# Opening and second group of a fused two-layer transformer step: blank products, spare buffers, loads and norm steps in other places

## The chip, the cores and the metric

The kernel runs on one core of a Trainium2 chip. A core has five engines with a queue of instructions each: TensorE (PE, matrix products; its weight loads are shown as PEld), VectorE (DVE), ScalarE (ACT), GpSimd (POOL) and SyncE (SP, which here only starts DMA transfers). The engines wait for each other through semaphores; within one queue the order is the order of the program. The metric is the device time of one execution in microseconds, lower is better. The kernel before takes 899.39 us (median of three runs, 898.83 to 901.31).

## What is computed

The reference takes x (64 sequences of 32 rows, width 256) and a context (64 x 257 rows) through two layers. Layer 0, where the change lies, is:

```python
x = x + _L0_xattn_ref(_layernorm(x, axis=-1), ctx_1024, ctx_1024, ...)   # windowed attention on the context
x = x + _L0_attn_ref(_layernorm(x, axis=-1), ...)                        # causal attention on x itself
x = x + _L0_ffn_ref(_layernorm(x, axis=-1), ...)                         # FP8 linear
```

Both attentions have 16 heads of 16 features and a rotary turn of queries and keys; each of the 32 query rows of a sequence sees at most 32 keys, so a layer 0 attention touches only the first 32 context rows. Layer 1 (attention on all 257 context rows, a gated mixer, and a mixture of experts) follows and isn't touched by the change.

## The kernel before, in words

The 2048 rows of x lie in four groups of 512 rows (`xs[0]` to `xs[3]`), each of four tiles of 128 rows. The function `small_attentions` runs both layer 0 attentions as eight steps, n = 0 to 7: the context attention of groups 0 to 3, then the self attention of groups 0 to 3. In this text "step n, tile t" is one turn of the inner loop. A turn does a piece of several jobs at once, so that PE always has something: it scores tile t of group n (`scores`), transposes and uses the exponentials of older tiles (`turned`, `context`, `by_feature`, `project`, on tiles one to four turns old), and prepares the next group `after`: `rotated` makes half of its keys (t = 0, 1) or queries (t = 2, 3), `values` its values (t = 0, 2).

`rotated` is the rotary turn: PE makes `ps_qk`; DVE makes `part` (sine part), SP starts four DMA transfers that move `part` by 32 partitions into `far`, `near` (cosine part) is made by ACT and POOL (by DVE in step 0's own opening), and POOL adds `near` and `far` into kT or qT. `spread_keys` copies kT into the block form `kb`. `v_rows`, `vb` carry the values through DRAM; `blocks` starts eight transfers a group.

The norm of a group is the generator `norm_steps`: statistics (`st`, four DVE instructions), aggregation (`mv`, then `ve`, `half`, `r`), three Newton rounds for the reciprocal root (`sq`, `rn`: nine small DVE instructions, or twelve on POOL), and four DVE instructions that write y. Its argument `eng` says which engine does the Newton rounds. Each `next` on the generator runs up to the next `yield`. `opened` transposes y on PE (eight `psT` products) and copies it with ACT into yT. Before the change, step n's loop works through the norm of group n + 2 in its four turns (`prepare`), with the Newton rounds on DVE for n = 0 and on POOL for n > 0, and opens that group in turn 3.

The order on every engine is the order of the program text in this part (`tc.keep_in_program_order`), and the rings of named buffers (`ring`) decide when a buffer comes free: `part` has two buffers, `near` two, `far` three, the PSUM banks of `pa` three. A DMA transfer also waits for the earlier transfer with the same one of eight semaphores.

The opening is what stands ahead of the loop: loads of x, weights, constants and context on SP's queue (`first_loads`), the norms of groups 0 and 1, the four rotations and the values of group 0.

Of the kernel before, what the change touches and what calls it, by code (L numbers as in the profile page):

```python
# [16 lines left out]
P = 128  # L17
# [48 lines left out]
def perceiver_kernel(ctx: ExitStack, tc: tile.TileContext, a: dict, out: bass.AP):  # L66
# [57 lines left out]
    def norm_steps(g, eng=None, apart=False, ts=range(NT), by_act=False, y=None):  # L124
# [18 lines left out]
        r = r0.bitcast(F32)  # L143
        for _ in range(3):
# [103 lines left out]
    def small_attentions(layers, first_loads, decode, sides, load_layer1, layer1):  # L248
# [30 lines left out]
        def clear(vb, engine):  # L279
            engine.memset(vb.rearrange("p b h g e -> p (b h g e)"), 0.0)  # L280
# [25 lines left out]
        def rotated(it, i, c):  # L306
# [19 lines left out]
            part = part_([P, GT], "part")  # L326
# [8 lines left out]
            near = near_([P, GT], "near")  # L335
# [166 lines left out]
        last = len(order) - 1  # L502
        in_order[0] = all_in_order[0] = True
# [9 lines left out]
        next(loads)  # L513
        for half in range(2):
            clear(vbs[0][half], vector)
            clear(vbs[1][half], gpsimd)
# [4 lines left out]
        adds = [rotated(it, 1, 0)]  # L521
        opened(it)
        mask(1)
        vector.tensor_tensor(eye, ident[:, 0:S], ident[:, 64 : 64 + S], ALU.add)
        steps = norm_steps(order[1][1], vector, apart=True)
        next(steps)
        adds.append(rotated(it, 1, 1))
# [4 lines left out]
        adds.append(rotated(it, 0, 1))  # L532
        adds[1]()
# [6 lines left out]
        after["y"] = finish(steps)  # L540
        for half in range(2):
            blocks(it, half)
        now = it


        line = [None] * 5
        adds = []
        layer1_loads = load_layer1()
        for n in range(len(order) + 1):
# [4 lines left out]
            kvT = coming = None  # L554
            if n + 2 <= last:
                side = norm_steps(order[n + 2][1], None if n else vector, apart=True)
            else:
                side = sides

            def prepare(at):  # L560
                if n + 2 <= last and at:
                    try:
                        next(side)
                    except StopIteration as end:
                        return end.value

            for t in range(NT):
# [12 lines left out]
                if t == 0:  # L580
# [11 lines left out]
                else:  # L592
                    y = prepare(t % 2 == 1)
                    adds.append(rotated(after, *((1, 0), (1, 1), (0, 0), (0, 1))[t]))
                    if (n, t) == (last - 1, NT - 1):
# [3 lines left out]
                prepare(t % 2 == 0)  # L599
# [6 lines left out]
                if n > 0 and (t % 2 == 0 or n + 2 > last):  # L606
# [7 lines left out]
                elif t % 2 == 0:  # L614
                    values(after, t // 2)
                    if (n, t) == (0, 0):
                        opened(after)
                elif t == 3:
                    for half in range(2):
                        blocks(after, half)  # L620
                    if n + 2 <= last:
                        coming = group(n + 2, kvT)
                        coming["y"] = y
# [1515 lines left out]
```

## Time and profile before

| what | value |
| --- | --- |
| median of three runs | 899.39 us (898.83 to 901.31) |
| profiled execution, its own time | 899.84 us |
| its span, first to last instruction | 898.1 us |
| mean granted TensorE clock | 0.984 |
| PE busy | 852.6 us (95%) |
| DVE busy | 577.4 us (64%) |
| POOL busy | 508.9 us (57%) |
| first scores read by DVE (`mx`, step 0, tile 0) | 33.33 us |
| step 1 from its first `part` (50.87) to that of step 2 (74.74) | 23.87 us |

Times are counted from the start of the span. The windows view gives busy time of each engine in a stretch and the clock that TensorE was granted; the chain of waits follows the last instruction back to the start and says for each stretch who set the end; the timeline lists instructions in order of time with their durations. Matrix products are pipelined, so PE's busy share counts waiting inside a product too.

### The profile page before, as it was taken

The numbers are of one execution on the slowest core, as the hardware profiler recorded it, in microseconds if no ns is written. First come the engines' busy times: TensorE is split into PE (matmuls) and PEld (weight loads), VectorE is DVE, ScalarE is ACT, GpSimd is POOL, SyncE is SP. The second block draws the span as 40 slices with busy tenths as digits, with TensorE's granted clock in tenths as the row PEclk, the third lists the DMA queues.
The fourth block names the chain that finished last, engine by engine and source line by source line (L and its number), as shares of the span: only waits on it lengthen the run. The fifth ranks groups of instructions, "written<-read, shape, count | busy, mean of one in ns | idle before, by whom it ended". The sixth has DMA issues, their size and how long they took to land.

```text
span 898.1 us, 22831 instructions
## 1 busy us (share of the span) xinstructions
PE 852.6 (95%) x8699; PEld 585.8 (65%) x8699; DVE 577.4 (64%) x1702; ACT 439.7 (49%) x1135; POOL 508.9 (57%) x990
## 2 busy tenths in 40 slices
PE   6899999987989999999999999999999889999996
PEld 3466666664556666666566665666676548888885
DVE  6887777895576767775787757776765861111116
ACT  2566667673455545555455554665653232222224
POOL 3477777773584657557475573685661254555430
PEclk9899999999999999999999999999998999999998
DMA  7455433543101111110111101120010056777768
GB/s 237 134 141 141 99 95 96 132 134 111 48 8 54 54 55 54 54 40 16 54 55 54 45 12 53 55 71 25 2 37 1 24 159 216 232 233 229 217 191 284
DMA packets 66926, 88.77 MB, mean 99 GB/s; under 512 B 32480, under 2 KB 50688, under 8 KB 64768
## 3 DMA queue, kind: packets, MB, share of 16 engines
q1 hardware_dynamic: 63264, 77.73, 28.8%
q0 software_dynamic: 3456, 9.44, 3.2%
q8 instruction: 69, 1.13, 0.6%
q14 instruction: 41, 0.34, 0.1%
q10 hardware_dynamic: 96, 0.13, 0.1%
HBM read 65.78 MB, written 13.11 MB: 88 GB/s over the span
## 4 chain that ended last, share of the span: by engine, by line
PE 72%; DVE 11%; POOL 6%; ACT 4%; issue 4%; DMA 3%; SPq 1%; DVEq 0%; POOLq 0%; ACTq 0%
PE ps_v L119 12%; PE ps_o L119 11%; PE ps_k L119 10%; PE ps_h L119 7%; PE ps_t L122 7%; PE ps_qk L119 5%; PE ps_s L119 3%; PE ps_p L119 3%; PE ps_so L119 2%; PE pair_bank L119 2%; PE ps_sh L119 2%; PE ps_q L119 2%; POOL sq L107 1%; POOL e L107 1%; ACT e L107 1%
## 5 line engine op out<-in xcount | busy, mean ns | idle before, releaser
L107 ACT ACTIVATE e<-e,xnm 128x257 f32<-128x257 f32 x256 | 127.2, 499 | 44.1 <-DVE xnm L107 39.5
L119 PE MATMUL ps_k<-ct,w_w_l1x 128*128 128x512 f32 x256 | 122.9, 602 | 3.5 <-DMA ct<-in_ctxT 2.4
L107 POOL TENSOR_SCALAR e<-e,xsm 128x256 f32<-128x256 f32 x256 | 124.2, 504 | 0.0
L107 DVE CUSTOM_DVE_ANT_0 e<-ps_s,mask 128x257 f32<-128x257 f32 x256 | 93.5, 421 | 43.7 <-PE ps_s L119 43.1
L119 PE MATMUL ps_v<-w_w_l1x,ct 128*128 128x256 f32 x512 | 121.1, 379 | 0.0
L122 PE MATMUL ps_t<-cst,e 128*128 128x128 f32 x640 | 102.1, 282 | 2.9 <-DVE eT L107 2.8
L119 PEld LDWEIGHTS ps_v<-w_w_l1x,ct 128*128 128x128 f32 x512 | 93.4, 190 | 10.9 <-ACT y L107 0.2
L107 DVE COPY eT<-ps_t 128x512 f32<-128x512 f32 x124 | 85.1, 686 | 23.4 <-PE ps_t L122 23.2
L107 ACT ACTIVATE kT<-ps_k,vec 128x512 f32<-128x512 f32 x64 | 44.0, 688 | 100.1 <-PE ps_k L119 100.1
L107 POOL TENSOR_TENSOR x<-x,rows 128x256 f32<-128x256 f32 x96 | 70.3, 750 | 34.5 <-DVE y L107 25.2
L122 PEld LDWEIGHTS ps_t<-cst,e 128*128 128x128 f32 x640 | 71.8, 141 | 20.8 <-DVE eT L107 4.4
L107 ACT ACTIVATE hTr<-ps_h,w 128x256 f32<-128x256 f32 (+1 forms) x80 | 31.4, 450 | 104.2 <-issue 90.5
L107 DVE TENSOR_TENSOR og<-ps_o,b 128x512 f32<-128x512 f32 (+1 forms) x20 | 12.8, 638 | 105.6 <-PE ps_o L119 105.6
L119 PEld LDWEIGHTS ps_k<-ct,w_w_l1x 128*128 128x128 f32 x256 | 44.6, 190 | 44.7 <-issue 36.8
L1882 POOL DMA_INDIRECT r_rows<-og,lv x36 | 35.6, 989 | 59.1 <-DVE og L107 54.2
L107 ACT COPY v<-ps_v 128x512 f32<-128x512 f32 x80 | 46.5, 582 | 41.6 <-PE ps_v L119 41.0
L119 PE MATMUL ps_h<-ygT,w 128*128 128x256 f32 (+1 forms) x320 | 65.8, 359 | 0.1
L119 PE MATMUL ps_o<-w,hTr 128*128 128x256 f32 x288 | 65.3, 379 | 0.0
L107 POOL TENSOR_TENSOR last<-e,xsm 128x4 f32<-128x4 f32 x64 | 15.4, 240 | 88.0 <-DVE xsm L107 86.5
L119 PEld LDWEIGHTS ps_o<-w,hTr 128*128 128x128 f32 x288 | 54.4, 190 | 7.2
L119 PEld LDWEIGHTS ps_h<-ygT,w 128*128 128x128 f32 x320 | 54.9, 190 | 6.2 <-issue 0.3
L107 ACT ACTIVATE kb<-kT,cst 128x256 f32<-128x256 f32 x96 | 45.4, 512 | 27.5 <-POOL kT L107 25.9
(223 smaller groups left out, 1668.9 us busy)
## 6 DMA issues: line engine op xcount, KB each, us to landing
ct<-in_ctxT SPq DMA_DIRECT2D x16, 1024.0 KB
w<-in_ew SPq DMA_DIRECT2D x20, 514.0 KB
w<-in_ew SPq DMA_DIRECT2D x20, 512.0 KB
far<-part SPq DMA_DIRECT2D x126, 64.0 KB
v_rows<-v SPq DMA_DIRECT2D x16, 256.0 KB
vb<-v_rows SPq DMA_DIRECT2D x64, 64.0 KB
r<-r_rows SPq DMA_DIRECT2D x8, 512.0 KB
b<-in_eb SPq DMA_DIRECT2D x20, 128.0 KB
```

What stands on the lines that cost most here:

```text
L107: ins = getattr(self.engine, name)(*args, **kw)
L119: return kept(nc.tensor.matmul(ps, **args))
L122: return kept(nc.tensor.transpose(ps, src, eye))
L1882: wrote = nc.gpsimd.indirect_dma_start(out=r_rows, out_offset=bass.IndirectOffsetOnAxis(ap=write_i[:, at : at + 1], axis=0), in_=o[:, i, : ...
```

## The change

The opening: a `blank` tile of zeros is written by DVE and 14 products of it are put ahead of PE's first real product. DVE's two clearings of `vb` go to POOL, which now clears all four. Both key rotations of group 0 come before `opened`, and they take their `part` and `near` from the tiles of the scores and exponentials (`spare`). The load of group 2's rows and of the last weight block moves from SP's queue early on to ACT's queue behind the second mask, that of group 3's rows and of one bias row to step 0, tile 2. The Newton rounds and y of group 1 come behind the query rotations (`split`).

The norms: group 2 does only its statistics in step 0 and the rest in step 1, turns 0 and 1, where it is opened; group 3 (in step 1) has its Newton rounds on DVE instead of POOL, its pieces in turns 1, 2 and 3. Group 1 is opened in step 0, turn 1 instead of turn 0. In step 0 the pending additions (`add`) come at the start of every turn. The fetch of group 2's context and one piece of the FP8 decoding come a turn or two later. From step 2 on the order of the turns is that of before.

```diff
...
     def turn(ps, src, eye):
...
-    def norm_steps(g, eng=None, apart=False, ts=range(NT), by_act=False, y=None):
+    def norm_steps(g, eng=None, apart=False, ts=range(NT), by_act=False, y=None, split=False):
...
         n, t0 = len(ts), ts[0]
...
         r0 = small.tile([P, n], I32, tag="r0", name="r0")
...
         r = r0.bitcast(F32)
+        if split:
+            yield
         for _ in range(3):
...
             rn = small.tile([P, n], F32, tag="rn", name="rn", bufs=6)
...
             scalar.copy(mk, cst[:, at : at + S][:, None, :].to_broadcast([P, 8, S]))
...
-        def clear(vb, engine):
-            engine.memset(vb.rearrange("p b h g e -> p (b h g e)"), 0.0)
+        def clear(vb):
+            gpsimd.memset(vb.rearrange("p b h g e -> p (b h g e)"), 0.0)
...
             layer, g = order[n]
...
                 return tile_.rearrange("p (b q) -> p b q", q=S)
...
             bias = vec[:, v0 + 2 * i + c : v0 + 2 * i + c + 1]
-            part = part_([P, GT], "part")
+            spare = (it["n"], i) == (0, 1)
+            part = sb.tile([P, GT], F32, tag=f"sc{c}", name="part") if spare else part_([P, GT], "part")
             vector.scalar_tensor_tensor(
...
             )
...
             for at in range(0, P, S):
...
                 queue.dma_start(out=far[at : at + S, :], in_=part[at ^ S : (at ^ S) + S, :])
-            near = near_([P, GT], "near")
+            near = sb.tile([P, GT], F32, tag=f"e{c}", name="near") if spare else near_([P, GT], "near")
             if it["n"] > 0:
...
                 gpsimd.tensor_tensor(by_seq(near), by_seq(near), by_place(cs), ALU.mult)
...
         last = len(order) - 1
+        blank = sb.tile([P, GT], BF16, tag="e2", name="blank")
+        vector.memset(blank, 0.0)
+        idle = psum.tile([P, GT], F32, tag="b5", name="idle")
+        for _ in range(14):
+            mm(idle, lhsT=blank[:, 0:P], rhs=blank, start=True, stop=True)
         in_order[0] = all_in_order[0] = True
...
         it = group(0, fetch(0))
...
         after = group(1, fetch(1))
-        next(loads)
-        for half in range(2):
-            clear(vbs[0][half], vector)
-            clear(vbs[1][half], gpsimd)
+        for vb in vbs[0] + vbs[1]:
+            clear(vb)
         scalar.copy(ident_bf, ident)
...
         it["kb"] = [None, None]
-        adds = [rotated(it, 1, 0)]
+        adds = [rotated(it, 1, c) for c in range(2)]
         opened(it)
         mask(1)
+        next(loads)
         vector.tensor_tensor(eye, ident[:, 0:S], ident[:, 64 : 64 + S], ALU.add)
-        steps = norm_steps(order[1][1], vector, apart=True)
+        steps = norm_steps(order[1][1], vector, apart=True, split=True)
         next(steps)
-        adds.append(rotated(it, 1, 1))
+        next(steps)
         adds[0]()
...
         adds.append(rotated(it, 0, 1))
+        next(steps)
         adds[1]()
...
             spread_keys(it, 0, 1, part)
...
             add()
...
             values(it, pair)
-        after["y"] = finish(steps)
         for half in range(2):
             blocks(it, half)
+        after["y"] = finish(steps)
         now = it
-
         line = [None] * 5
-        adds = []
+        adds, side = [], None
         layer1_loads = load_layer1()
...
             if n > 0:
...
             if after is not None:
...
             kvT = coming = None
+            earlier = side
             if n + 2 <= last:
-                side = norm_steps(order[n + 2][1], None if n else vector, apart=True)
+                side = norm_steps(
+                    order[n + 2][1], None if n > 1 else vector, apart=True, split=n == 0
+                )
             else:
...
-            def prepare(at):
-                if n + 2 <= last and at:
+            def prepare(count):
+                y = None
+                for _ in range(count if n + 2 <= last else 0):
                     try:
...
                     except StopIteration as end:
-                        return end.value
+                        y = end.value
+                return y
+
+            ahead, behind = {
+                0: ((0, 0, 0, 0), (0, 0, 1, 0)),
+                1: ((0, 0, 0, 1), (0, 1, 1, 0)),
+            }.get(n, ((0, 1, 0, 1), (1, 0, 1, 0)))
...
                 if (n, t) == (last + 1, 2):
...
                     elif after is not None:
...
                 due, adds = adds, []
-                if t == 0:
+                if t == 0 or n == 0:
                     for add in due:
...
                     due = []
...
                 if after is None:
...
                 else:
-                    y = prepare(t % 2 == 1)
+                    if n == 1 and t == 0:
+                        next(earlier)
+                    elif n == 1 and t == 1:
+                        after["y"] = finish(earlier)
+                    y = prepare(ahead[t])
                     adds.append(rotated(after, *((1, 0), (1, 1), (0, 0), (0, 1))[t]))
+                    if n < 2 and t == 1:
+                        opened(after)
                     if (n, t) == (last - 1, NT - 1):
...
                     by_feature(line[3])
-                prepare(t % 2 == 0)
+                prepare(behind[t])
+                if (n, t) == (1, 0):
+                    next(earlier)
                 if n + 2 > last:
...
                     add_bias(n - 1, t)
-                if n > 0 and (t % 2 == 0 or n + 2 > last):
+                if n > 0 and (n, t) != (1, 0) and (t % 2 == 0 or n + 2 > last):
                     next(decode, None)
...
                     add()
...
                     next(layer1, None)
...
                     values(after, t // 2)
-                    if (n, t) == (0, 0):
-                        opened(after)
                 elif t == 3:
...
                         coming = group(n + 2, kvT)
-                        coming["y"] = y
-                        opened(coming)
+                        if n > 0:
+                            coming["y"] = y
+                            opened(coming)
                 line[0] = scores(now, t) if n <= last else None
...
                     pair_pool.close()
...
                     sums(line[1])
...
                     next(side, None)
-                if t == 0 and n + 2 <= last:
+                if (n, t) == (1, 0):
+                    next(earlier)
+                elif (n, t) == (1, 2):
+                    prepare(1)
+                if t == (0 if n else 1) and n <= last - 2:
                     kvT = fetch(n + 2)
-                elif n < 3:
+                elif n < 3 and (n, t) != (0, 0):
                     next(loads, None)
...
                     next(layer1_loads, None)
...
             sync.dma_start(out=w_cur[:, i], in_=a["w_l0x"][:, i])
...
         yield
-        sync.dma_start(out=xs[2], in_=x_view[2])
-        sync.dma_start(out=w_cur[:, 3], in_=a["w_l0x"][:, 3])
+        scalar.dma_start(out=xs[2], in_=x_view[2])
+        scalar.dma_start(out=w_cur[:, 3], in_=a["w_l0x"][:, 3])
+        yield
+        sync.dma_start(out=xs[3], in_=x_view[3])
         row_load(R_XO0)
-        sync.dma_start(out=xs[3], in_=x_view[3])
         yield
         sync.dma_start(out=raw, in_=a["w_fp8"])
-        for at in (R_AO0, R_FF, R_XO1, R_GO):
+        row_load(R_AO0)
+        for at in (R_FF, R_XO1, R_GO):
             yield
```

## The prediction

> **What bounds the kernel now.** I read the page's busy times first, then busy time by stretch, then the chain of waits, then the timeline at the places that the change moves.
>
> ```profile
> PE 852.6 (95%) x8699; PEld 585.8 (65%) x8699; DVE 577.4 (64%) x1702; ACT 439.7 (49%) x1135; POOL 508.9 (57%) x990
> ```
>
> PE sets the time almost everywhere, so only time in which PE has nothing to do, or runs at half clock, can be won. The next view has step 1 and step 2, each from its first `part` to that of the next step (columns: PE, weight loads, DVE, ACT, POOL busy, granted clock, DMA share, GB/s).
>
> ```profile
> 50.87:74.74 23.87, 23.23 (x370) 16.09 (x369) 20.02 (x45) 15.79 (x37) 17.93 (x29) 1.00 0.53 131
> 74.74:98.57 23.83, 23.50 (x370) 16.01 (x369) 18.41 (x44) 16.25 (x37) 17.14 (x29) 1.00 0.54 138
> ```
>
> The reader is to see that step 1 has 0.64 us of idle PE, but that DVE, the engine to which the change sends work, is at 20.02 of 23.87, with 3.85 us left, and POOL at 17.93.
>
> ```profile
> 26.50:30.00 3.50, 1.39 (x7) 0.64 (x5) 3.29 (x12) 0.00 (x0) 0.69 (x2) 0.99 0.58 167
> 30.00:33.40 3.40, 2.51 (x45) 1.76 (x46) 1.44 (x6) 2.93 (x6) 1.74 (x2) 0.50 0.57 134
> 33.40:36.80 3.40, 3.40 (x4) 0.90 (x4) 3.06 (x15) 1.03 (x2) 0.00 (x0) 0.50 0.65 190
> ```
>
> After a stretch with PE at 40% the granted clock is half for 6.8 us. The chain of waits has what that and the opening cost:
>
> ```profile
> 13.70 5.26 DMA far<-part
> ...
> 27.20 2.95 issue
> ...
> 33.20 3.71 PE ps_qk L119 x4
> ...
> 38.18 1.72 PE ps_qk L119 x4
> ```
>
> The first `far` needs 5.26 us, behind rows that nobody needs yet. ACT then waits 2.95 us at 27.20 for the `part` of group 1, which stands on DVE behind group 1's Newton rounds and y. The same four products take 3.71 us at half clock and 1.72 later. The timeline shows what holds those rounds, DVE first, then POOL:
>
> ```profile
> 24.09 0.16 DVE L107 SCALAR_TENSOR_TENSOR sq<-sq,ve 128x4 f32<-128x4 f32 x1
> 24.29 1.24 DVE L107 SCALAR_TENSOR_TENSOR rn<-sq,r 128x4 f32<-128x4 f32 x1
> 25.56 1.19 DVE L107 TENSOR_TENSOR sq<-rn 128x4 f32<-128x4 f32 x1
> 26.79 0.41 DVE L107 SCALAR_TENSOR_TENSOR sq<-sq,ve 128x4 f32<-128x4 f32 x1
> 27.23 0.16 DVE L107 SCALAR_TENSOR_TENSOR rn<-sq,rn 128x4 f32<-128x4 f32 x1
> ```
>
> ```profile
> 24.24 2.49 POOL L107 TENSOR_TENSOR qT<-near,far 128x512 f32<-128x512 f32 x2 [1.48 <-DMA far<-part]
> 26.71 0.48 POOL L107 TENSOR_SCALAR kb<-kT,cst 128x256 f32<-128x256 f32 x1
> ```
>
> A Newton instruction of 0.16 us that meets a POOL instruction ends with it: 1.24 and 1.19 us beside the two additions, 0.41 beside `kb`. Just one passes between two POOL instructions. In step 1 POOL is full right behind the `part` that ends at 51.62:
>
> ```profile
> 51.83 0.47 POOL L107 TENSOR_SCALAR kb<-kT,cst 128x256 f32<-128x256 f32 x1
> 52.51 1.28 POOL L107 TENSOR_TENSOR near<-near,cst 128x512 f32<-128x512 f32 x1 [0.21 <-ACT near L107]
> 53.74 0.92 POOL L107 TENSOR_TENSOR x<-x,rows 128x256 f32<-128x256 f32 x1
> 54.64 0.48 POOL L107 TENSOR_SCALAR kb<-kT,cst 128x256 f32<-128x256 f32 x1
> ```
>
> **The opening, up to the first scores.** DVE's clearings (two of 1.76 us) go. Group 0's statistics start at 5.06 behind them; SP's issue at 4.75, which waits for the landing of the same rows, says that they could start 0.3 us earlier. From there to y's end the trace takes 5.42 us. POOL now clears four times 1.81 us, to 7.97, and `ve`, `half`, `r` come at 6.4. No row has such a DVE instruction beside a clearing: 0 if they pass, 1.6 if they wait to 7.97; the nearest row, a y of 0.69 instead of 0.35 us beside a POOL addition, waits, but that addition reads and a clearing doesn't, so I take the middle, 0.8. y ends at 11.0 (10.2 to 11.8; before 10.48).
>
> By the Trainium skill, "SBUF — State Buffer", "Who interferes with whom", the first to issue of a two-port DVE instruction and any GpSimd instruction holds the shared ports to its end; these three could be such instructions, and by it the sum would be 0.8 us worse. No row here shows it.
>
> DVE then has two `part` and two `near` of the keys (4 x 0.67), eye, statistics, aggregation (2.4), and `part`, `near`, `part` of the queries (2.0): the last ends at 18.1 instead of 21.80. The 14 blanks run beside all this: PE is free until the context's rows land (6.89). Each lies between 0.27 us (bf16 128x256, warm) and 0.86 (f32 128x512, half clock); at 0.43, half of the latter, they end at 7.6 and delay keys that DVE reads from 11.0: nothing. Cover gone (0.86 each, to 13.6), up to 2.6 us.
>
> On the queues, ACT issues group 2's rows and the weight block behind its second mask copy at about 14; with some 3.5 us to landing (step 0's context, issued at 34.72, landed so) that is 17.5, and SP's first `far` of the queries reuses that transfer's semaphore. Then four issues and two of 0.63 us, 1.6 to landing (issue ends 48.93, addition starts 50.58), and POOL's second addition of 1.27: qT is there at 24.5, the second half of the scores (0.35) and `mx` at 24.9. Group 1's `r` can meet POOL's first kT addition, up to 1.27; I take 0.8 and have `mx` at 25.7 instead of 33.33. Bounds 24.9 and, with y's 0.8 more, 27.
>
> From there to the first `part` of step 1 PE has 15.7 us at the full-clock rows (four turns: `ps_qk` 1.72 four times, `ps_v` 1.73, scores 0.69 three times, group 1's eight `psT` 0.97, and the small ones). Two new waits come, the second `psT` bank and `ps_qk` for yT, both on ACT: 1.3 and 0.9; eight hand-overs of 0.05 make 0.4. Before, the same stretch took 17.54 with 2 us of half clock and group 2's `psT`. `part` comes at 43.9 instead of 50.87: **-7.0** (-5 to -8.5).
>
> **Step 1.** Call that `part` P. In turn 0: part 0.67; nine Newton instructions at 0.20, 1.8; their waits, each POOL instruction holding one of them (rest of qT's addition 0.3, kb 0.47, near 1.28, x 0.74, kb 0.48): 3.3. mx, sc, o, sums: 2.63; y 0.67, x 0.30, y 0.67. y ends at P+10.0. PE stands before the second half of `psT`; then `psT` 0.48, `ps_c` 0.22, scores 0.69; behind part and group 3's statistics `mx` comes at P+12.0, before at P+7.6: 4.4 lost.
>
> In turn 1 to 2: ACT's near, two yT and cT behind `part` (P+10.7) end at P+13.1, `ps_p` and `ps_qk` at 15.7, part 16.4, aggregation 17.3, Newton 1.8 plus near 1.28, x 0.74, kT 1.28, kb 0.5, less the 0.3 that overlaps: 22.6; the CAST 0.29 (its 1.22 at 52.85 ends 0.28 behind POOL's near). `mx` at P+22.9, before P+14.7. Turn 3 and the first of step 2: mx to y 4.27, `psT`, scores 1.2, ps_o to scores 6.4: P+34.8, before P+26.6. Step 1 loses **+8.2**, of which 6.8 are POOL's holds. 3.4 us of Newton on POOL go, which hid at all but 0.64 us.
>
> PE now stands twice for about 3 us. After 40% busy the row above has half clock. If a low stretch follows here, PE's work of a turn (5 to 6 us) takes up to 3.4 us more, twice, partly beside DVE: 0 to 5, I take **+2.5**. By the Trainium skill, "TensorE: Matmul & The Clock Gate", "What's actually happening", a whole idle window of about 3.4 us is needed, so that stands of 3 us would cost nothing and the sum be +1.2; the row at 26.50, 1.39 of 3.50 busy, speaks against it.
>
> From step 2 on the turns are those of before and PE is full: nothing moves. The later decode step and loads are hidden: DVE has 5 us free in step 2, and the eighth product's weights come in step 4. Sum: -7.0 + 8.2 + 2.5 = +3.7. The profiled execution's own time is 899.84 (span 898.1; 0.45 above the median): **903.5 us**.
>
> **Rivals.** (1) The lead stays. If POOL stands behind a late `far` while DVE does its rounds, they pass at 0.20 each; then step 1 loses the added work alone, 8.2 - 6.8 = 1.4, plus 0.8 for the clock, and the sum is -4.8: 895.0. For it: POOL is idle 6 us of 23.87, and qT's addition waited 0.72 for `far` at 50.58. Against it: near and x follow every `part` within 1.6 us. It decides once the holds fall under 3.0 us. (2) No clock loss: -7.0 + 8.2 = +1.2, 901.0. For it: the two stands are shorter than the 3.5 us stretch. (3) The opening gives half: y waits, and ACT's load lands late, so the queries' `far` stand on SP: -4.5 + 8.2 + 4 = +7.7, 907.5, with half clock in the opening as well.
>
> **How the numbers follow.** Forecast 44%, (1) 27%, (2) 14%, (3) 15%. What a measurement can tell here is about 0.3%, 2.7 us: faster is below 896.7, slower above 902.1. (1) gives faster 0.25 and the rest same; (2) gives same with a quarter slower; the forecast and (3) give slower but for 0.03: faster 0.25, same 0.16, slower 0.59. Range 894.0 to 908.5, which leaves out the best of (1) and the worst of (3); the forecast's own is 901.5 to 907.
>
> **What would show it.** First `mx` at 25 to 27; no half clock near 30; Newton instructions of 0.4 to 1.3 us on DVE in step 1; step 1 (first `part` to the next step's) 32 to 35 us instead of 23.87, with PE idle for about 3 us before `psT` in turn 1 and before `ps_c` in turn 3; windows of 0.50 behind these. Wrong if step 1 stays under 27 us, or if the first scores come after 29.

## The result, and the profile after

The changed kernel takes 904.74 us (median of nine runs, 902.43 to 908.38) against 899.44 us; the ratio is 1.0061, with a 95% interval of 1.0041 to 1.0082. It is slower, by about 5 us. The profiled execution took 903.56 us, with a span of 901.8 us. Its busy times, from the page:

```profile
PE 859.8 (95%) x8713; PEld 589.2 (65%) x8713; DVE 580.9 (64%) x1710; ACT 439.3 (49%) x1135; POOL 508.1 (56%) x980
```

The page's sums tell little, so busy time by stretch is to be read. Step 1 and step 2 of the changed kernel, each from its first `part` to that of the next step (columns as in the prediction):

```profile
45.87:75.45 29.58, 24.68 (x373) 16.12 (x372) 25.84 (x67) 16.76 (x38) 15.00 (x17) 1.00 0.43 110
75.45:99.67 24.22, 23.50 (x370) 16.02 (x369) 19.43 (x44) 16.28 (x38) 18.21 (x29) 1.00 0.52 142
```

Step 1 grew from 23.87 to 29.58 us: DVE is busy for 25.84 of it (before 20.02), and PE has 4.9 us to spare instead of 0.64. The granted clock is 1.00, so in this execution none of it is the clock. The stretch that had the half clock before:

```profile
26.50:30.00 3.50, 3.01 (x23) 1.60 (x12) 2.82 (x5) 2.54 (x6) 1.27 (x1) 1.00 0.38 88
30.00:33.40 3.40, 2.87 (x50) 1.66 (x49) 2.23 (x4) 3.40 (x8) 0.00 (x0) 1.00 0.55 127
33.40:36.80 3.40, 2.89 (x50) 1.89 (x48) 2.06 (x5) 0.94 (x3) 1.97 (x3) 1.00 0.58 157
```

The half clock there is gone. Where the time went, in four readings of DVE's timeline:

| | before | changed | difference |
| --- | --- | --- | --- |
| first scores read (`mx`, step 0, turn 0) | 33.33 | 27.30 | -6.0 |
| first `part` of step 1 | 50.87 | 45.87 | -5.0 |
| first `part` of step 2 | 74.74 | 75.45 | +0.7 |
| first `part` of step 3 | 98.57 | 99.67 | +1.1 |
| end of the span | 898.1 | 901.8 | +3.7 |

The opening wins 5 us, step 1 loses 5.7, step 2 another 0.4. The rest comes late: from 250 us on both kernels run the same instructions in the same order on PE, DVE, ACT and POOL, and yet 1.7 us are lost near 617 and 1.8 near 710, while 0.8 come back between 200 and 250 us. At both places the changed kernel's clock records have a half-clock window more (3.41 us each). The profiles of the experiments show that such windows come and go though the work there is the same (last section). So this trace places only 1.1 of the 3.7 us in the steps that the change touches.

The chain of waits of this trace reaches back only to 892.95 us, so the waits view has to stand for it. For PE from 26 to 76 us, the three longest (who waited for whom; us in total, times, longest):

```profile
PE ps_c L122 <- DVE o L107: 1.9, 1, 1.9
PE pair_bank L119 <- POOL qT L107: 1.8, 1, 1.8
PE psT L122 <- DVE y L107: 0.9, 2, 0.7
```

Before, PE had three such waits (1.5, 1.5 and 0.6 us), in step 0 and behind turn 1 of step 1. The first of the new ones is DVE's fourth-group rounds in turn 2 of step 1. The timeline there, POOL and DVE together:

```profile
61.40 1.27 POOL L107 TENSOR_TENSOR near<-near,cst 128x512 f32<-128x512 f32 x1 [2.19 <-ACT near L107]
61.47 1.23 DVE L107 TENSOR_TENSOR sq<-r 128x4 f32<-128x4 f32 x1
...
63.31 1.27 POOL L107 TENSOR_TENSOR kT<-near,far 128x512 f32<-128x512 f32 x1
63.41 1.19 DVE L107 SCALAR_TENSOR_TENSOR rn<-sq,r 128x4 f32<-128x4 f32 x1
```

Each of these rounds starts behind the beginning of a POOL instruction and ends with it; the one between them, beside POOL's `x`, takes 0.65 us. The scores of that turn lie ready in PSUM from 62.4 on and are read at 66.21. The second wait, of 1.8 us, is another thing: a qT addition at 47.85 that waited 2.44 us for `far`, because the load of group 3's rows was put at 40.97 among the small transfers. The DMA view from 40 to 50 us (KB each, median us from issue to landing):

```profile
x<-in_x SPq DMA_DIRECT2D x1, 512.0 KB
...
far<-part SPq DMA_DIRECT2D x4, 64.0 KB, 4.5
```

From 30 to 34 us, with no load beside it, the same view gives 2.0 for a `far`. An experiment further down bears out that the load is the cause: with it elsewhere PE's wait for qT falls from 1.8 to 0.2 us.

### The profile page after: what moved, and what is told of

Its sections match the earlier page's. It is cut to its first block, busy times and chain, and to the rows that moved or that the text cites. A ratio compares the mean times of both kernels' runs of the same rounds, so it can differ in the third digit from the quotient of the medians.

```text
span 901.8 us, 22853 instructions
## 1 busy us (share of the span) xinstructions
PE 859.8 (95%) x8713; PEld 589.2 (65%) x8713; DVE 580.9 (64%) x1710; ACT 439.3 (49%) x1135; POOL 508.1 (56%) x980
```

## Experiments

All ratios are to the kernel before, run on the same chip in the same series; brackets hold 95% intervals. "Turn" is a turn of the step's inner loop, `mx` the moment at which DVE reads that turn's scores.

### The two halves of the change by themselves

The opening alone: the changed kernel's opening, loads and additions, with the norms in the loop as before.

```diff
-                side = norm_steps(
-                    order[n + 2][1], None if n > 1 else vector, apart=True, split=n == 0
-                )
+                side = norm_steps(order[n + 2][1], None if n else vector, apart=True)
...
-            ahead, behind = {
-                0: ((0, 0, 0, 0), (0, 0, 1, 0)),
-                1: ((0, 0, 0, 1), (0, 1, 1, 0)),
-            }.get(n, ((0, 1, 0, 1), (1, 0, 1, 0)))
+            ahead, behind = (0, 1, 0, 1), (1, 0, 1, 0)
...
-                        if n > 0:
-                            coming["y"] = y
-                            opened(coming)
+                        coming["y"] = y
+                        opened(coming)
...
```

> The changed kernel's opening, loads and additions, with the norms of the steps as they were before (third group's whole norm in step 0 on VectorE, fourth group's Newton rounds on POOL in step 1). Theory A (the opening wins 6 us and the moved norms lose 7 in step 1): first scores read by VectorE at 27.3 as in the changed kernel, first part of step 2 at 92.5 to 94 instead of 98.57, time 894 (ratio 0.994). Rival B (what the opening wins is lost again by step 2 whatever the norms do, since step 0 then waits for its loads): first scores at 27.3, first part of step 2 within 1 us of 98.57, time 899.4 (ratio 1.000). Rival C (the blank products and the earlier start put one or two more half-clock windows behind step 8, 3.5 us in the profile of the changed kernel, whatever the steps do): steps as by A, but time 897.5 (ratio 0.998).

Measured: 904.62 us, ratio 1.0039 [1.0013, 1.0065]. First scores at 28.77. The expectation's reading has to be mended: its 98.57 is the kernel before's first `part` of step 3, not of step 2, and 92.5 to 94 was meant for that one. It came at 101.95 (and that of step 2 at 77.77, 3.0 later than before), so none of the three holds. It isn't a clean half, either. Group 2's rounds now stand in turn 1 in front of a `part`, and group 1's yT, which ACT copies behind that `part`, is late:

```profile
PE ps_qk L119 <- ACT yT L107: 3.9, 1, 3.9
```

```profile
30.64:34.06 3.42, 0.93 (x28) 0.49 (x15) 2.98 (x14) 0.91 (x3) 0.00 (x0) 1.00 0.53 121
34.06:37.47 3.41, 2.03 (x3) 1.00 (x4) 1.72 (x4) 3.41 (x8) 1.90 (x3) 0.50 0.61 163
```

PE stands 3.9 us (first view: waits), and the clock is half for 6.8 us behind that (second: windows). By turn 2 the whole lead of 4.6 us is gone. So rival B in another form: here the opening's gain does not outlast the group 2 norm that DVE has to do in step 0.

The norms alone: the opening and the loads of before, with the changed kernel's norms in the loop.

> The opening and loads of before, with the changed kernel's norms in the steps. Theory A: the moved norms alone lose 7 us between the first scores of step 0 and those of step 2 (43.5 to 45 us there in the kernel before, 51.27 in the changed one), time 906.5 (ratio 1.008). Rival B (the loss in the changed kernel belongs to the early start, for example to transfers that are not there yet, and not to the norms): the same stretch within 1.5 us of that before, time 899 to 901 (ratio 1.000 to 1.002). Rival D (the loss is half and half): 903 (1.004).

Measured: 909.25 us, ratio 1.0078 [1.0046, 1.0110]; from the first scores of step 0 to those of step 2 51.86 us (before 44.12, changed 51.27). So between those readings the norms cost 7.7 us with the opening of before, and 7.2 with the changed one: theory A's 7 us whatever the opening does, and rivals B and D fall. Half clock is part of these numbers (3.4 us of that stretch before, 8.9 here, none in the changed kernel), so they are no pure price of DVE's work. The time is above theory A's 906.5. The rounds are held here as in the changed kernel (1.27, 0.41 and 1.22 us in turn 0; 1.23, 0.66, 1.19 in turn 2). The profile has the half clock behind turn 2's stand as well, which the changed kernel's has not:

```profile
68.90:72.31 3.41, 1.53 (x5) 0.39 (x3) 3.24 (x10) 0.72 (x2) 0.21 (x1) 1.00 0.15 46
72.31:75.72 3.41, 2.73 (x33) 1.88 (x40) 2.62 (x8) 1.45 (x4) 0.00 (x0) 0.50 0.00 0
```

### Another engine: the rounds on POOL

Both groups', and then the fourth group's alone:

```diff
-order[n + 2][1], None if n > 1 else vector, apart=True, split=n == 0
+order[n + 2][1], None, apart=True, split=n == 0                      # both
+order[n + 2][1], None if n else vector, apart=True, split=n == 0     # the fourth group's alone
```

> The changed kernel with all Newton rounds of the third and fourth group on POOL (12 instructions of 0.2 us a group), in the same places of the order. Theory A in its prediction's form (POOL's holds on VectorE's Newton instructions are most of the loss, about 5 us of long instructions in the profile of the changed kernel): mx of turn 2 of step 1 at about 61 to 62 instead of 66.21, time 899.5 to 901 (ratio 1.000 to 1.002). Rival E (it is the place of the norms, not the engine: statistics, rounds, y and transposes of the third group all in step 1 have to pass in a row): no gain, 904.5 (ratio 1.006); where POOL is full, even 906.

> The changed kernel with the fourth group's Newton rounds alone on POOL, as before; the third group's stay on VectorE in step 1. Theory A: turn 2 of step 1 is freed of 1.8 us of work and some 2.5 us of holds on VectorE, turn 0 keeps its own; mx of turn 2 comes 3 to 4 us earlier than 66.21, time 901 (ratio 1.002). Rival E (place, not engine): 904.5 (1.006). Rival F (POOL's rounds of the fourth group stand behind its near, x and kT additions and come no sooner than VectorE's): mx of turn 2 at 65 to 66, 904.

Measured: 905.34 us, 1.0041 [1.0018, 1.0063], and 904.75 us, 1.0036 [1.0008, 1.0064]. With both groups on POOL `mx` of turn 2 comes at 64.93, not at theory A's 61 to 62, and the time is rival E's. The second run shows why taking the rounds off DVE doesn't give the time back. `mx` of turn 2 comes at 62.45, the 3.8 us earlier that theory A said. But the next turn, from there to its own `mx`, takes 8.1 us instead of 5.6:

```profile
65.92 0.20 POOL L107 TENSOR_TENSOR rn<-sq,rn 128x4 f32<-128x4 f32 x1
66.07 0.72 POOL L107 TENSOR_TENSOR x<-x,rows 128x256 f32<-128x256 f32 x1
66.15 2.06 DVE L107 TENSOR_SCALAR y<-x,mv,rn 128x256 f32<-128x256 f32 x2 [1.08 <-POOL rn L107]
66.75 1.31 POOL L107 TENSOR_TENSOR kT<-near,far 128x512 f32<-128x512 f32 x1
```

Twelve rounds on POOL end at 66.12, y waits for them, is itself held by the two POOL instructions behind (2.06 instead of 0.64 us), and the transposes of turn 3 wait for y. Of 3.8 us, 1.2 are left at the first `part` of step 2 (74.26). So rival E has a share: the changed kernel begins this norm a turn later than the kernel before did, and no engine has room to catch up.

### Other places

Group 2's norm back into step 0, in its turns 1 to 3, and group 3's with the rounds on POOL, as before:

```diff
-                    order[n + 2][1], None if n > 1 else vector, apart=True, split=n == 0
+                    order[n + 2][1], None if n else vector, apart=True, split=n == 0
...
-                0: ((0, 0, 0, 0), (0, 0, 1, 0)),
-                1: ((0, 0, 0, 1), (0, 1, 1, 0)),
+                0: ((0, 0, 1, 0), (0, 1, 1, 0)),
...
-                if (n, t) == (1, 0):
-                    next(earlier)
-                elif (n, t) == (1, 2):
-                    prepare(1)
+                if (n, t) == (0, 3):
+                    prepare(1)
+                elif (n, t) == (1, 0):
+                    after["y"] = finish(earlier)
```

> The changed kernel with the third group's statistics in turn 1, its Newton rounds in turn 2 and its first y at the end of turn 3 of step 0 (all on VectorE), the second y in turn 0 of step 1, and the fourth group's norm as before: statistics in turn 0, rounds on POOL in turn 1, y in turns 2 and 3. Theory E (it is the places: in the changed kernel the third group's rounds stand before the scores of turn 0, and the fourth group's norm begins a turn later than before and is late for the transposes of turn 3): first part of step 2 at 71 to 72.5 instead of 75.45, time 900.5 to 901.5 (ratio to before 1.000). Rival A2 (VectorE has no room in step 0 either, step 0 gets longer by what step 1 gets shorter): first part of step 1 at 48 to 49 instead of 45.87, that of step 2 at 74 to 75.5, 904 (1.004).

Measured: 903.31 us, 1.0028 [1.0007, 1.0049]. Step 1 takes 25.07 us, 4.5 less than in the changed kernel, but begins at 50.73 instead of 45.87, and step 2 at 75.80: rival A2, a little beyond its own figures. The nine rounds in turn 2 of step 0 take 5.6 us instead of 1.8, and six of them are held; behind that stand the clock is half from 42.3 to 49.2 us, which has its part in step 1's late begin:

```profile
36.63 1.24 DVE L107 SCALAR_TENSOR_TENSOR rn<-sq,r 128x4 f32<-128x4 f32 x1
...
38.10 1.12 DVE L107 SCALAR_TENSOR_TENSOR sq<-sq,ve 128x4 f32<-128x4 f32 x1
...
39.70 1.21 DVE L107 TENSOR_TENSOR sq<-rn 128x4 f32<-128x4 f32 x1
```

### Loads, blank products, clearing

The loads of groups 2 and 3 and of the last weight block together on SP, behind the queries' last `far`:

```diff
         mask(1)
-        next(loads)
...
         adds.append(rotated(it, 0, 1))
+        next(loads)
...
-        scalar.dma_start(out=xs[2], in_=x_view[2])
-        scalar.dma_start(out=w_cur[:, 3], in_=a["w_l0x"][:, 3])
-        yield
+        sync.dma_start(out=xs[2], in_=x_view[2])
+        sync.dma_start(out=w_cur[:, 3], in_=a["w_l0x"][:, 3])
         sync.dma_start(out=xs[3], in_=x_view[3])
+        yield
```

> The changed kernel with the third and fourth group's rows and the last weight block issued together on SP behind the queries' last far, instead of on ACT at 13.5 and on SP at 41. Theory G (large transfers that land between the small far ones cost the changed kernel part of its gain: far takes 4.1 to 4.6 us there instead of 1.4, the first kT addition starts at 18.75 when its last far lands at 18.73, and in turn 0 of step 1 PE stands 1.8 us for a qT addition whose far takes 3.1 to 3.5 us): first kT addition at 16.5, first scores read at 25 to 25.7 instead of 27.30, mx of turn 0 of step 1 at 46 to 47 instead of 49.73, time 2 to 3.5 us below the changed kernel, 902 (ratio to before 1.001). Rival H (VectorE's y of the second group and its Newton rounds bound the first scores anyway, and what is won is lost in step 1 to the norms): first scores at 27, part of step 2 within 1 us of 75.4, 904.7 (1.004 to 1.005).

Measured: 909.51 us, 1.0113 [1.0081, 1.0145], the slowest of all. Half of theory G is right: first scores come at 25.73, so the loads at 13.5 do cost the changed kernel's opening 1.6 us. But these 1.25 MB now lie in front of the writes of v to DRAM, and ACT can't refill v:

```profile
30.57 0.59 ACT L107 COPY v<-ps_v 128x512 f32<-128x512 f32 x1 [3.18 <-DMA v_rows<-v]
```

PE waits 3.4 us for that copy, and turn 1 takes 6.9 us instead of 3.6. Neither place was free. This run shows one thing more. In step 1 the last qT addition waits only 0.75 us for its `far` (2.44 in the changed kernel), POOL is busy while DVE does its rounds in turn 0, and five of the nine are held, for 3.0 us together; PE stands before `psT` in turn 1 and before `ps_c` in turn 3, and the clock is half behind both (waits, then the windows at the first stand; at the second they are 70.64 to 77.46):

```profile
PE psT L122 <- DVE y L107: 2.9, 2, 2.2
PE ps_c L122 <- DVE o L107: 1.9, 1, 1.9
```

```profile
53.58:56.99 3.41, 1.19 (x4) 0.18 (x3) 3.31 (x10) 1.51 (x3) 0.00 (x0) 1.00 0.65 178
56.99:60.40 3.41, 3.41 (x50) 2.35 (x51) 2.87 (x8) 1.74 (x4) 0.97 (x1) 0.50 0.66 183
```

Step 1 takes 32.65 us here.

Both of these edits, with the second pair of buffers cleared in turn 0 of step 0:

> Both of these edits, and the clearing of the second pair of buffers moved from the start to turn 0 of step 0 on POOL (the clearing holds ve at 6.35 for 1.27 us). Theories E and G together: first scores at 24 to 25, first part of step 2 at 68 to 70, time 896 to 898 (ratio 0.995 to 0.997). Rivals: with E alone 900 (1.000), with neither 904 (1.004).

Measured: 903.88 us, 1.0035 [1.0014, 1.0055]. First scores at 24.96, 8.4 us ahead of the kernel before; both losses, that of v and that of the rounds, follow. Step 1 begins at 51.45 and step 2 at 76.52, where 68 to 70 was said.

Without the blank products:

```diff
-        for _ in range(14):
-            mm(idle, lhsT=blank[:, 0:P], rhs=blank, start=True, stop=True)
```

> The changed kernel without the 14 blank products and the buffer that they read. Theory I (they raise the clock before the first products: the eight products of the keys take 3.67 us at full clock, at half clock 3.4 to 7.3): first part 1.7 us later than 11.31, first far and first scores 1.5 to 3 us later than 27.30, time 906.5 to 907.5 (ratio to before 1.007). Rival J (VectorE's statistics, rounds and y of the first group bound the first part anyway, which comes behind a y that ends at 11.39): first scores within 0.7 us of 27.30, time 904.7 (1.005).

Measured: 905.29 us, 1.0062 [1.0042, 1.0083], and first scores at 27.25: rival J. The keys' products take 5.39 us instead of 3.67, but the first `part` stays at 11.34 behind DVE's y. At that place the blank products neither win nor cost anything that these runs show.

### The rounds in the same places, but not held

The rounds' `ve` and square in the unused half of the scores' PSUM banks, for groups 2 and 3:

```diff
+        if bank:
+            ve, psq = (shared[0][:, i, D : D + n] for i in range(2))
...
-            if eng is vector:
+            if bank:
+                vector.tensor_tensor(psq, ve, r, ALU.mult)
+                vector.scalar_tensor_tensor(psq, psq, -0.5, r, ALU.mult, ALU.mult)
+                vector.scalar_tensor_tensor(rn, psq, 1.5, r, ALU.add, ALU.mult)
+            elif eng is vector:
                 vector.tensor_tensor(sq, r, r, ALU.mult)
...
-            pair_bank = pair_psum.tile([P, 2, 512], F32, tag="b34", name="pair_bank")
+            pair_bank = shared[0]
```

> The changed kernel with two of the Newton rounds' operands of the third and fourth group (ve and the square) in the unused half of the scores' PSUM banks, so that each round's instruction reads one operand from PSUM and one from SBUF; the same instructions, order and engines otherwise (the products of r are grouped differently). A sc or part, which read PSUM, were never held by POOL in the traces. Theory A (POOL's holds on instructions that read two operands from SBUF are what makes the rounds long): no round over 0.25 us, mx of turn 2 of step 1 at 63.5 to 64.5 instead of 66.21 (2.7 us of holds go in turn 2, 0.5 to 1 comes back since the scores now share the banks; those in turn 0 are hidden behind a qT addition that waits for far until 47.64), first part of step 2 at 72.5 to 73.5 instead of 75.45, time 901.5 to 902.5 (ratio to before 1.002). Rival E (it is the places): first part of step 2 at 75 to 76, 904.7 (1.005). Rival K (POOL holds instructions with a PSUM operand as well): rounds as long as before.

Measured: 901.97 us, 1.0021 [1.0000, 1.0042]. The rounds beside POOL's `near` of turn 2, DVE first, then POOL:

```profile
63.35 0.17 DVE L107 TENSOR_TENSOR pair_bank<-pair_bank,r 128x4 f32<-128x4 f32 x1
63.55 0.17 DVE L107 SCALAR_TENSOR_TENSOR pair_bank<-pair_bank,r 128x4 f32<-128x4 f32 x1
63.76 0.16 DVE L107 SCALAR_TENSOR_TENSOR rn<-pair_bank,r 128x4 f32<-128x4 f32 x1
```

```profile
63.29 1.26 POOL L107 TENSOR_TENSOR near<-near,cst 128x512 f32<-128x512 f32 x1 [2.19 <-ACT near L107]
```

None of the 18 rounds takes over 0.17 us; before the edit one such instruction ended with every POOL instruction it met. So the holds are real, and those of the rounds belong to two operands from SBUF; rival K falls. The Trainium skill, "SBUF — State Buffer", "Who interferes with whom", says the same: a VectorE instruction with at most one SBUF input, outside the two-port modes, doesn't contend with GpSimd. An instruction with a single operand can be held too, where it reads and writes SBUF: `r` takes 1.10 us in turn 0 of this run, and `ve` took 1.23 at 44.20 in the changed kernel, just ahead of step 1. The stretch from `mx` of turn 1 to that of turn 2 falls from 10.43 to 8.37 us. What comes back is a wait of PE for the last round (2.8 us in two places), as the scores' products write the same banks. By the Trainium skill, "PSUM — Partial Sum Buffer", "PSUM bank collisions raise a hardware error", two engines must not be in one bank and partition quadrant at once even at other addresses, and the ordering that the build puts there fits it; no run here tried it without.

Theory A's readings of the timeline don't hold: `mx` of turn 2 comes at 66.05 and the first `part` of step 2 at 75.30, as rival E has it. This execution had a half-clock window behind the stand before turn 0's scores (50.5 to 53.9 us), to which the shared banks belong; the next run, without such a window, has 73.09 for step 2. The times are theory A's, and by them about two thirds of the loss are gone (ratio 1.0021 instead of 1.0061, in different series).

All four groups so:

> The same for all four groups of the first steps, the opening's two included. Theory A: ve of the first group 0.2 instead of 1.44 us, y of the first group ends at 10.2 instead of 11.39, that of the second at 23 to 24 instead of 26.7; first scores read at 25.2 to 26 instead of 27.30, where the products then bound them; step 1 as in the kernel with the two groups alone; time 900 to 901 (ratio to before 1.000). Rival L (far, which lands at 18.73, bounds the opening): first scores within 0.7 us of 27.30 and the time that of the kernel with two groups.

Measured: 901.49 us, 1.0008 [0.9983, 1.0032]. y of group 1 ends at 23.9 and first scores come at 26.48, first `part` of step 2 at 73.09, with `far` (first kT addition at 18.50) now in front: theory A and rival L each in part. The hold on group 1 went on to y, which reads and writes SBUF (3.30 us instead of 1.4). In group 0 the hold only went on by one instruction: `ve`, which writes PSUM, takes 0.17, and `r`, which reads and writes SBUF, 1.01 us to the end of the clearing.

The same in the kernel before:

> The kernel before with the same PSUM operands for the three groups whose rounds VectorE does, and nothing else. Theory A: the second group's rounds at 24.09 to 27.39 take 1.8 instead of 4 us, the first part of the second group is ready 2 us earlier than 29.32, first scores at 30.5 to 31.5 instead of 33.33, first part of step 1 at 47.5 to 49.5 instead of 50.87 (where PE's window is then over half full, the half clock at 30 to 36.8 goes too), time 896 to 898.5 (ratio to before 0.996). Rival M (the opening there is bound by far and by the order of the queue, and the rounds are hidden): 900.5 (1.000).

Measured: 899.66 us, 0.9988 [0.9971, 1.0005], between theory A and rival M and not clear of 1. First scores come at 31.59 and step 2 at 73.59, 1.7 and 1.2 us earlier than before. One half-clock window is left of two, but in turn 1 PE waits for the last round, which uses the shared banks:

```profile
35.76 0.30 PE L119 MATMUL pair_bank<-mk,eye 64*32 64x256 bf16 x8 [1.86 <-DVE rn L107]
```

### A version that beats both

From these readings: the kernel before, with PSUM operands for group 1's rounds alone (those that the qT additions held), and blank products where PE stood and the clock really dropped, two and seven before the halves of group 1's transposes.

```diff
-        steps = norm_steps(order[1][1], vector, apart=True)
+        steps = norm_steps(order[1][1], vector, apart=True, bank=True)
...
         for pair in range(y.shape[1] // 2):
+            if fill:
+                fill(2 + 5 * pair)      # products of a blank tile into a free bank
...
-                        opened(after)
+                        opened(after, blanks)
```

> The kernel before with two edits: the second group's Newton rounds with PSUM operands (that group alone), and two and seven blank products before the two halves of its transposes, where PE stood 1.5 and 1.5 us. Theory N (what the changed kernel's opening was worth can be had at that place: the rounds are not held by the qT additions, and a window that was busy 40 to 43% is filled, so that the half clock at 30 to 36.8 does not come): first scores read at 30 to 30.8 instead of 33.33 with no granted clock of 0.50 there, first part of step 1 at 47.3 to 48.3 instead of 50.87, that of step 2 at 71.2 to 72.5 instead of 74.74, time 896.5 to 898 (ratio to before 0.996 to 0.997). Rival O (the clock's drop costs the path nothing, since turn 0 waits for far): 899.7, as with the PSUM operands alone (0.999). Rival P (the blank products stand in the way of the transposes): 900.5 or more.

Measured: 897.76 us against 901.73, ratio 0.9959 [0.9935, 0.9983]: theory N. PE's timeline at that place, and the windows:

```profile
25.91 0.59 PE L119 MATMUL idle<-blank 128*128 128x512 bf16 x2
26.34 0.60 PE L122 MATMUL psT<-cst,y 128*128 128x128 f32 x4
26.77 1.67 PE L119 MATMUL idle<-blank 128*128 128x512 bf16 x7
28.46 0.66 PE L122 MATMUL psT<-cst,y 128*128 128x128 f32 x4
```

```profile
26.50:30.00 3.50, 3.49 (x56) 2.03 (x56) 2.53 (x8) 2.29 (x5) 1.52 (x2) 1.00 0.46 106
30.00:33.40 3.40, 3.40 (x50) 1.73 (x50) 3.06 (x15) 1.67 (x4) 0.22 (x1) 1.00 0.40 91
```

The clock stays at 1.00, first scores come at 29.91, step 1 begins at 47.44 and step 2 at 70.92, 3.8 us earlier than before. The mean granted clock over the runs is 0.987, against 0.984 of the kernel before. What each of the two edits gives alone wasn't run. The PSUM operands for three groups gave 0.9988, but with a wait of 1.9 us in turn 1 that isn't here, so the part of the blank products in the 0.4% isn't shown.

## Why the prediction was right, and where it wasn't

It said 903.5 us and slower; 904.74 was measured. The mechanism was right: what the opening wins is lost again in step 1, where POOL holds DVE's rounds. That the profiled span grew by just the 3.7 us of the sum is luck. Up to the first `part` of step 3 this trace loses 1.1 us; the rest are windows of half clock near 617 and 710 us, less 0.8 won back between 200 and 250, and the prediction had nothing there. By the runs the change costs 3.7 to 7.4 us, and no trace says where all of it lies.

**The opening, -7.0 said, -5.0 measured,** at the end of its range. The stretch from first scores to step 1 was sized well (18.2 said, 18.57 measured); the first scores came 1.6 us late (27.30; 25.7 said). Two terms were too small. The first is the landing of transfers: ACT's load was given some 3.5 us and no effect on the keys' `far`. From 13 to 14.9 us (median us from issue to landing; a `far` alone has 2.0):

```profile
far<-part SPq DMA_DIRECT2D x4, 64.0 KB, 4.6
w_w_l0x<-in_w_l0x ACTq DMA_DIRECT2D x1, 256.0 KB, 5.8
```

POOL's first kT addition starts at 18.75, and with the loads on SP behind the last `far` at 16.19; the first scores then come at 25.73, where they were forecast. The second is the 0.8 us for group 1's rounds. They met five POOL instructions, and then y met two:

```profile
19.23 0.81 DVE L107 TENSOR_TENSOR sq<-r 128x4 f32<-128x4 f32 x1
20.84 1.27 DVE L107 SCALAR_TENSOR_TENSOR sq<-sq,ve 128x4 f32<-128x4 f32 x1
22.91 1.12 DVE L107 SCALAR_TENSOR_TENSOR rn<-sq,rn 128x4 f32<-128x4 f32 x1
24.07 2.64 DVE L107 TENSOR_SCALAR y<-x,mv,rn 128x256 f32<-128x256 f32 x4
```

Against 0.16 each and 1.4 for y the holds come to 4.3 us (3.1 on the rounds, the two shorter ones among them, and 1.2 on y), not 0.8. Not much of it reached the first scores: PSUM operands for the rounds brought them 0.8 us forward (26.48). The clearing held `ve` for 1.27 us (1.44 instead of 0.17), inside the 0 to 1.6 that was given, and y ended at 11.39 instead of 11.0. `ve` ended at 7.79, with the clearing (7.78): so far the trace agrees with the Trainium skill's rule on the two-port forms ("SBUF — State Buffer", "Who interferes with whom"). The blank products cost nothing, as said.

**Step 1, +8.2 said, +5.7 measured.** Behind the first `part` at P, `mx` was said at P+12.0 in turn 1, P+22.9 in turn 2 and P+34.8 in the first turn of step 2; it came at P+9.9, P+20.3 and P+32.7. The mis-sized term is the holds: 6.8 said, one for every POOL instruction from `part` on; 4.1 measured (1.06 and 0.25 in turn 0; 1.07, 0.49, 1.03 and 0.17 in turn 2, all over the bare 0.16). In turn 0 most rounds ran at 0.16, because POOL stood behind a late `far`: rival 1's mechanism, for one turn. That `far` stood behind the moved load of group 3's rows, a transfer that the prediction counted as hidden ("The later decode step and loads are hidden"). That sentence was wrong, and so PE stood before the scores of turn 0 and not before `psT` in turn 1. How much the holds of turn 0 cost isn't shown, as PE waited there for the same qT addition; turn 2 takes 3.4 us longer than before, and its holds are 2.8. The place was right in turn 3 (before `ps_c`, behind turn 2's rounds: 1.9 us; 3 were said).

With the loads together on SP that `far` isn't late, and step 1 is the one forecast: 3.0 us of holds in turn 0 (3.3 said), 2.2 us before `psT`, half clock behind both stands, `mx` at P+12.2, P+22.3 and P+35.8, 32.65 us in all (32 to 35 said).

**The clock, +2.5 said.** In the profiled execution no window from 6.8 to 201 us is at half clock, as rival 2 has it; windows of 0.50 behind the stands do come in the runs with the norms alone and with the loads together. Over the runs the mean is 0.9816 in nine runs of the changed kernel and 0.9840 in thirty of the kernel before in another series. One window of 3.41 us at half clock takes 0.0019 off the mean of 900 us; so 1.3 windows, 2.2 us of PE's time, near the 2.5. But single runs of the changed kernel lie between 0.977 and 0.986, and without the blank products the mean is 0.983. So the size isn't shown, nor that those windows lie behind step 1's stands.

**Rival 1** (the lead stays if the holds are under 3.0) fell, with 4.1; with the holds on the rounds of all four groups removed the change breaks even (1.0008), short of the 895 us that it gave. Rival 3 (the opening gives half) was nearer in the opening's size, -4.5 against -5.0, and ACT's load did land late; its half clock in the opening did not come, and its 907.5 is too much.

Two terms too large and of opposite sign, off by 2.0 and 2.5, hid each other: luck as well. What the runs do show is the trade: the norms alone cost 7 us, and without the holds on the rounds of groups 2 and 3 two thirds of the loss go.

## What to carry to other kernels

Before small work is moved to an engine that has free time in the profile, look whether its instructions read two SBUF operands beside another engine's long ones: here 0.16 us became up to 1.27, and one operand in PSUM was enough to end that. Two limits showed: the next instruction from SBUF to SBUF was held in its place, and a bank that TensorE writes too made TensorE wait, 2.8 us in one run. A lead in the opening is worth only what the next queue doesn't take back, so follow it to the first turn at which the order of work is the old one again. And fill a stand of TensorE where the clock really drops, not where a kernel happens to begin: 14 blank products at the start gave nothing; nine in the gap before a drop were part of a version that wins 0.4%, though their own share wasn't measured.

## What the runs showed of the hardware

**Same instructions, other clock.** All kernels here run identical work from 250 us on. Near 617 us ten of the fourteen profiles have a half-clock window of 3.41 us and four have none, where PE's rows are busy throughout; each such window costs 1.5 to 1.7 us of the span. In all, from 13.6 to 885 us, the profiles, one for each kernel, have between 13.7 and 37.5 us at half clock. So a single profiled span says little within 3 us; the readings up to 100 us and the mean clock of many runs say more.

**Busy share and clock.** A window that PE was busy for 1.54 of 3.41 us kept the full clock behind it, and one that was busy for 1.96 lost it, as did one of 1.53 (the norms alone). The first two lines are of the changed kernel, the other two of that with both groups' rounds on POOL (each pair: a window and the next):

```profile
64.78:68.19 3.41, 1.54 (x6) 0.47 (x4) 3.20 (x11) 0.54 (x1) 0.38 (x1) 1.00 0.25 59
68.19:71.60 3.41, 2.54 (x53) 1.42 (x52) 2.80 (x8) 1.45 (x4) 0.00 (x0) 1.00 0.00 0
```

```profile
69.15:72.56 3.41, 1.96 (x40) 1.27 (x47) 3.16 (x6) 0.66 (x2) 1.86 (x3) 1.00 0.08 16
72.56:75.97 3.41, 3.41 (x71) 2.68 (x51) 2.56 (x5) 3.41 (x9) 2.79 (x3) 0.50 0.34 77
```

So PE's busy share alone doesn't decide in these rows; what does stays open. Windows with less of it all went one way: each that PE was busy for under 1.4 us, from 13 to 250 us in the fourteen profiles, was followed by half clock. By the Trainium skill, "TensorE: Matmul & The Clock Gate", "What's actually happening", it takes an idle window; none of these was idle.

**Loads among small transfers.** In the changed kernel a `far` of 64 KB landed 2.0 us after the start of its issue when no load was beside it, 4.5 behind a load of 512 KB on its own queue, and 4.6 beside one on ACT's queue (medians).
